# A start with x in order on one queue and TensorE filled, a reordered sixth pair, and scan results ahead of additions in the last part

## The chip, the cores and the metric

The kernel runs on one core of a Trainium2 chip. The metric is the device time of one execution in microseconds (us). Three runs of the kernel before gave 1817.42, 1815.12 and 1814.30 us; their median, 1815.12 us, is the time before.

## The reference

The input x has 4 images of 128 channels and 96 x 96 points. Each image is normalized in 32 groups of 4 channels (mean and variance over the group's channels and all points). The normalized image is read as four sequences of 9216 points: by rows, by rows backwards, by columns, by columns backwards. Each sequence goes through one block with the same weights:

```
t = grouped1x1(x, in_proj, 4 groups)            # 128 -> 512 channels
u, gate = t[:256], t[256:]
u = conv1d(silu(u), 5 taps, each channel by itself)
s = ssm_in u;  bb = tanh(B u);  cc = tanh(C u)  # 32 channels each
a = DMIN + (DMAX - DMIN) * sigmoid(delta u)
h[l] = a[l] * h[l-1] + bb[l] * s[l]             # a scan along the sequence
u = u + ssm_out (cc * h + d * s)
y = out_proj (grouped1x1(u * sigmoid(gate), mix))
```

The four results are put back into image order, joined to 512 channels, multiplied with fuse_w (128 x 512), and x is added.

## The kernel before, in words

**Tiling.** The work is cut into 384 units. Two units, s = 0 (forward) and s = 1 (backward), make a pair, and `pair(t)` is called for t = 0 to 191. A batch element has two phases of 24 pairs: V (by columns) and H (by rows). A phase has 6 steps (st) of 4 pairs (p, or k). A unit covers 384 points (every fourth point of 16 lines). In the first three steps of a phase (`fresh`) the input projection and the gates are computed; in the last three the forward and backward units change places and the stored results are read back from DRAM (`load_silu`, `load_kept`).

**One pair.** `pair(t)` (line 784 on) has a front part for units 2t and 2t+1 and a back part for the pair LAG = 6 earlier, so that pairs 0 to 5 have no back part and pair 6 is the first that has one. On TensorE the order is: `front` (the input projection `in_proj` of the step after, four products into four PSUM banks, followed by four Silu on ScalarE, line 470), `conv` and `conv_less` (the convolution of half of the channels as products with diagonal matrices), an `accumulate` of a finished unit (the product with w_fin, line 729 on), `gates_and_out` (gates line 491, scan result times ssm_out line 504), a second `accumulate`, and `proj` (the products with w_proj). The other half of the channels is convolved on VectorE: `taps`, tap 0 on ScalarE (line 635) and taps 1 to 4 on VectorE (line 637), all through one pair of PSUM banks. `recurrence` does the scan on VectorE (line 709, two halves per step) and `outputs` (lines 715 and 716, then a copy) multiplies it by cc and adds the d * s term on GpSimd; d * s is `scale_s` on ScalarE (line 692). `gating` (lines 583 and 584) multiplies with the gate on VectorE. `sigmoids` (line 521) evaluates the gates on ScalarE. `accumulate` ends in an addition into `acc` (line 761), which is the output image of the batch element, held in SBUF and preloaded with x: on GpSimd from a copy `ys`, or on VectorE straight from PSUM where `direct` is set.

**What sets the order.** The program runs under a manual schedule: each engine executes its instructions in the order in which the program text issues them. SyncE (SP) issues nearly all DMAs in that order on one queue.

**The opening**, `start()` (line 996) and the lines before it. `load_x` (line 294) asks for the first image in ten DMAs of 1, 1, 1, 2, 2, 3, 4, 4, 4 and 2 chunks of 384 points, with one `bn_stats` on VectorE per chunk (line 298). After these come the weights `fuse` (512 KB) and `main` (384 KB), two loads of `x_in` for step 0 (385 KB each) and eight for the gates, all on SP's queue; only `small` is asked for from ScalarE. `stats_finish(b0)` turns the statistics into the scaled weights `wn` and biases `bn` over four small products, with TensorE kept busy by `filler` products (line 1000) and by the products `outer` (line 1007) and `inner` (line 1015), from which w_fin is made. Then sixteen Silu, one per s, block j and g, in the order of j = 0 and then j = 1, with two buffers of `x_in` that serve step 0 and step 1 alike, so that the loads of step 1 (`load_rows`) follow the products of step 0. `proj(0)` issues the front of step 1 itself.

**Statistics of later images.** `chunks_of` (line 372) names the chunks of the next image that a V pair loads and gives to `bn_stats` (line 387): two in each pair with k of 2 or 3, in all six steps, with four buffers `xs`.

**The end**, `tail()` (line 905): for the last six pairs (first = 186) it issues gating, the last scan, four `outputs`, and an alternation of `product`, `add` and `ssm_out`.

Of the kernel before, what the change touches and what calls it, by code (L numbers as in the profile page):

```python
# [67 lines left out]
def conv_preact_kernel(  # L68
# [18 lines left out]
    accf = acc.rearrange("p h r m -> p (h r m)")  # L87
    x_in = [big.tile([P, R, N + 1], F32, name=f"x_in{s}") for s in range(2)]
# [65 lines left out]
    gmask = wp.tile([P, 4], F32, name="gmask")  # L154
    nc.gpsimd.memset(gmask, 1.0)
# [13 lines left out]
    stats, free = {}, [FRONT[1]]  # L169
# [10 lines left out]
    def stats_finish(b):  # L180
# [12 lines left out]
        nc.vector.tensor_copy(mean, pm[:, 0:1])  # L193
        dev = sp.tile([P, 1], F32, tag="dev", name=f"dev_{b}")
        nc.vector.tensor_sub(dev, mv[:, 0:1], mean)
        ex = sp.tile([P, 1], F32, tag="ex", name=f"ex_{b}")
        nc.vector.scalar_tensor_tensor(ex, dev, dev, mv[:, 1:2], ALU.mult, ALU.add)
        gm4 = sp.tile([P, 4], F32, tag="gm4", name=f"gm4_{b}")
        nc.vector.tensor_scalar_mul(gm4, gmask, mean)
# [9 lines left out]
        if b == b0:  # L209
# [4 lines left out]
            nc.vector.reciprocal(inv, std)  # L214
        else:
# [11 lines left out]
        yield  # L227
# [11 lines left out]
        product(pb[:, 0:4], wn, gm4)  # L239
        if b == b0:  # L240
            for g in range(4):
                for q in range(R):
                    mm(pb[:, 4 + g : 5 + g], q, wn[0:32, 32 * g : 32 * g + 32], mean[0:32, :], True, True)
            nc.vector.tensor_sub(bn, b_in, pb[:, 0:8])
        else:
# [10 lines left out]
        nc.vector.tensor_scalar_mul(bn[:, 2:4], bn[:, 2:4], 0.5)  # L256
# [8 lines left out]

    def load_front(step, s, r, q):
        if fresh(step):
            un = units[step * UB + s]
            nc.sync.dma_start(
                x_in[s][r, q, :], xs[un["b"], un["lay"], r, q, bass.ds(un["st"] * N, N + 1)]  # L270
            )
# [22 lines left out]
    def load_x(chunks):  # L294
        for c, n in chunks:
            nc.sync.dma_start(accf[:, bass.ds(c * SC, n * SC)], xr[b0, :, bass.ds(c * SC, n * SC)])
            for e in range(c, c + n):
                nc.vector.bn_stats(stats_of(b0)[:, e, :], accf[:, bass.ts(e, SC)])
# [6 lines left out]
    nc.scalar.activation(first_table, first_table, AF.Sqrt)  # L305
    w_small = load(small, "small", nc.scalar)
    load_x([(0, 1), (1, 1), (2, 1), (3, 2), (5, 2), (7, 3), (10, 4), (14, 4), (18, 4), (22, 2)])
    w_out_fuse = load(fuse, "fuse")
    w_main = load(main, "main")
    for s in range(2):  # L310
        load_front(0, s, half(s), slice(0, R))
    for i in range(UB):
        load_gate(i)
# [29 lines left out]
    for s in range(2):  # L343
# [14 lines left out]
    nc.gpsimd.tensor_scalar_mul(  # L358
        w_proj[:, :, 2 * MH : 3 * MH], w_proj[:, :, 2 * MH : 3 * MH], 0.5
    )  # L360
# [3 lines left out]
    gates = [wk.tile([P, 2, 2, N], F32, tag=f"gate{e}", bufs=1, name=f"gate{e}") for e in range(2)]  # L364
# [7 lines left out]
    def chunks_of(t):  # L372

        un = units[2 * t]
        b, k = un["b"] + 1, t % R
        if un["order"] == "V" and b < B and k > 1:
            return [(b, un["st"] * R + 2 * (k - 2) + e) for e in range(2)]
        return []

    def load_chunks(t):  # L380
        for b, c in chunks_of(t):
            chunks[b, c] = wk.tile([P, SC], F32, tag="xs", bufs=4, name=f"xs_{b}_{c}")
# [78 lines left out]
    def in_proj(step, g, s, j, bk):  # L461
        wn = stats[units[step * UB]["b"]][0]
        r = slice(64 * s + 32 * j, 64 * s + 32 * j + 32)
        for c in range(4):
            m, q = (c, g) if j else (g, R - 1 - c if s else c)
            mm(bank(bk), c, wn[r, s, 32 * m : 32 * m + 32], x_in[s][r, q, :], True, True)

    def silu(step, g, s, j, bk):
# [3 lines left out]
            bank(bk)[:, : N + 1],  # L472
            AF.Silu,
# [40 lines left out]
    def sigmoids(bi, to):  # L514
# [3 lines left out]
        for s in range(2):  # L518

            for j in (0, 1) if s == 0 or to[0] == GATE[True][0] else (1, 0):  # L520
# [30 lines left out]
    def gates_and_out(bi, with_front):  # L551

        to = GATE[with_front]
# [19 lines left out]
    def gating(bi, s):  # L573
# [8 lines left out]
        if bi not in seeded:  # L582
            nc.vector.tensor_add(pz, pz, v)
# [13 lines left out]
    def conv(i, banks):  # L597
# [3 lines left out]
        for s in range(2):  # L601
# [21 lines left out]
    def taps(i, ks, first=None):  # L623
# [4 lines left out]
        part = psum[:, TAPS : TAPS + 2, :N]  # L628
        for k in ks:
# [6 lines left out]
            else:  # L636
                nc.vector.scalar_tensor_tensor(  # L637
                    us[i][:, :, 1, :] if k == K - 1 else part,
# [9 lines left out]

    def proj(i, banks, apart=False):
# [8 lines left out]
        turns = [(e, j) for j in ((1, 0) if i else (0, 1)) for e in range(2)]  # L658
        apart = apart or not i
        for e, j in sorted(turns) if apart and i else turns:  # L660
            if i == 0 and (e, j) == (0, 0):
                first = front_parts(R, (5, 4, 2, 3), half=True)
                next(first)
                next(first)
                first_tap(2)
                for _ in first:
                    pass
            for c, cols in enumerate(((qb, qb, qa, qa), (qs, qs, qc, qc))[e]):
                first, end = (j == 0, j == 1) if apart else (j == 1, j == 0)
                mm(bank(banks[e]), c, w_proj[:, j, cols], us[i][:, c % 2, j, :], first, end)  # L670
# [19 lines left out]
    def scale_s(i):  # L690
        s = tbs[i][0:64, :]
        nc.scalar.activation(s, s, AF.Copy, scale=d_sb[0:64, 0:1])
# [91 lines left out]
    def pair(t):  # L784
# [13 lines left out]
        if back:  # L798
# [13 lines left out]
        if t:  # L812
            new_u(i)
            taps(i, range(1, K))
            conv(i, banks)
        if t and not ahead:
            conv_less(i, banks)
        if not back and t:
# [86 lines left out]
    def tail():  # L905
# [35 lines left out]
        ssm_out(first + 1)  # L941
        for held_add in adds:
# [3 lines left out]
        outputs(2 * first + 8, None)  # L946
# [4 lines left out]
        outputs(2 * first + 10, None)  # L951
# [44 lines left out]
    def start():  # L996
        w_of = wp.tile([P, 4, 2, P], F32, name="w_of")

        def filler(n):
            nc.tensor.matmul(  # L1000
                bank(7)[:, :n], accf[:, bass.ds(10 * SC, P)], accf[:, bass.ds(10 * SC, n)],
# [3 lines left out]
        def outer(d, i, copy):  # L1005
# [175 lines left out]
```

## Time and profile before

| what | us |
|---|---|
| median of three runs | 1815.12 |
| the profiled execution's own time | 1815.66 |
| its span, first to last instruction | 1813.9 |
| TensorE busy | 1788.7 |
| ScalarE busy | 1562.6 |
| VectorE busy | 1448.5 |
| GpSimd busy | 1431.1 |
| granted TensorE clock, mean | 0.999 |

The span is one profiled execution; 1.8 us of its own time lie outside it. A group of instructions has a line of the kernel, an engine, what it writes and reads, a shape, how often it ran, its busy time, and the idle time ahead of it with what ended that. PE is TensorE, PEld its weight loads, DVE VectorE, ACT ScalarE, POOL GpSimd, SP SyncE. TensorE is nearly always busy in this page, but the ends of matrix products are modelled, so idle time of TensorE is better read from the start times of successive products.

### The profile page before, as it was taken

How to read it: one execution, taken by the hardware profiler on the slowest of the kernel's cores; microseconds unless marked ns; L12 is line 12 of the kernel's file. 1: busy time of each engine (PE TensorE's matmuls, PEld its weight loads, DVE VectorE, ACT ScalarE, POOL GpSimd, SP SyncE). 2: the span in 40 equal slices, each digit the busy share in tenths (PEclk: the TensorE clock that was granted, in tenths of full speed). 3: DMA queues.
4: the chain of work that ended last, by engine and by line, in shares of the span. 5: the costliest groups of instructions: out<-in, count | busy, mean ns of one | idle time of the engine just before them, and what ended most of it. 6: DMA issues, size and time to landing. Idle time of an engine off the chain costs nothing.

```text
span 1813.9 us, 56969 instructions
## 1 busy us (share of the span) xinstructions
PE 1788.7 (99%) x24090; PEld 643.7 (35%) x24090; DVE 1448.5 (80%) x1462; ACT 1562.6 (86%) x2750; POOL 1431.1 (79%) x1477
## 2 busy tenths in 40 slices
PE   7999999999999999999999999999999999999998
PEld 3333333333333333333333333333333333333333
DVE  6888878787888887877778888787877788777886
ACT  4888888988888888898888888889888888888975
POOL 3587888788778888787877888878877788887786
PEclk9999999999999999999999999999999999999999
DMA  8555463444975466344696456443476634635434
GB/s 247 178 188 180 148 195 107 162 144 155 314 239 186 158 186 183 113 139 139 221 300 226 144 176 207 127 164 118 159 237 220 232 142 138 197 102 180 149 123 158
DMA packets 148047, 321.17 MB, mean 177 GB/s; under 512 B 14160, under 2 KB 115920, under 8 KB 147792
## 3 DMA queue, kind: packets, MB, share of 16 engines
q1 hardware_dynamic: 147648, 317.48, 54.1%
q8 instruction: 190, 3.11, 0.7%
q14 instruction: 65, 0.53, 0.1%
q10 hardware_dynamic: 144, 0.04, 0.0%
HBM read 185.21 MB, written 132.25 MB: 175 GB/s over the span
## 4 chain that ended last, share of the span: by engine, by line
PE 94%; DVE 2%; DMA 2%; ACT 1%; issue 0%; POOL 0%; SPq 0%; DVEq 0%; ACTq 0%; POOLq 0%
PE psum L134 81%; PE psum L504 8%; PE psum L491 5%; DVE psum L637 1%; DMA x_in<-in_xs 1%; DMA xs<-in_xr 1%; DVE u L584 0%; DMA acc<-in_xr 0%; DVE u L637 0%; ACT psum L635 0%; ACT psum L512 0%; ACT u L618 0%; ACT sil L470 0%; DVE t L715 0%; DVE t L709 0%
## 5 line engine op out<-in xcount | busy, mean ns | idle before, releaser
L637 DVE SCALAR_TENSOR_TENSOR psum<-sil,small,psum 128x768 f32<-128x768 f32 x576 | 589.0, 1022 | 28.3 <-ACT psum L635 3.4
L584 DVE SCALAR_TENSOR_TENSOR u<-gate,psum 128x768 f32<-128x768 f32 x376 | 349.6, 952 | 273.9 <-ACT u L616 122.4
L134 PE MATMUL psum<-u,w_fin 128*32 128x384 f32 (+1 forms) x6192 | 552.7, 486 | 3.5 <-DVE acc L761 2.1
L134 PE MATMUL psum<-u,main 128*32 128x384 f32 x6144 | 534.7, 489 | 1.2 <-DVE u L637 1.2
L761 POOL TENSOR_TENSOR acc<-ys,acc 128x384 f32<-128x384 f32 x375 | 411.7, 1119 | 27.9 <-ACT ys L744 8.4
L715 POOL TENSOR_TENSOR t<-t,t 64x384 f32<-64x384 f32 (+1 forms) x192 | 237.3, 1236 | 157.0 <-DVE t L709 73.3
L134 PEld LDWEIGHTS psum<-u,w_fin 128*32 128x32 f32 x6192 | 189.7, 110 | 322.6 <-issue 215.2
L134 PEld LDWEIGHTS psum<-u,main 128*32 128x32 f32 x6144 | 181.9, 109 | 324.5 <-issue 196.8
L512 ACT COPY psum<-u 128x768 f32<-128x768 f32 x352 | 276.8, 799 | 19.2 <-DVE u L637 11.3
L134 PE MATMUL psum<-sil,band 128*32 128x384 f32 x3072 | 285.1, 488 | 0.0
L682 POOL TENSOR_SCALAR t<-tm 64x384 f32<-64x384 f32 x191 | 177.0, 926 | 118.1 <-ACT tm L674 98.9
L716 POOL TENSOR_TENSOR t<-t,t 64x384 f32<-64x384 f32 (+1 forms) x192 | 248.8, 1296 | 15.1
L504 PE MATMUL psum<-t,main 32*128 32x384 f32 x1536 | 239.2, 513 | 1.3 <-ACT psum L512 0.6
L635 ACT ACTIVATE psum<-sil,small 128x768 f32<-128x768 f32 x191 | 173.2, 907 | 58.0 <-DVE u L584 49.7
L521 ACT ACTIVATE gate<-psum,bnorm 128x384 f32<-128x384 f32 x384 | 191.7, 581 | 27.0 <-PE psum L491 25.5
L683 POOL TENSOR_TENSOR t<-t,tm 64x384 f32<-64x384 f32 x192 | 195.1, 1016 | 15.3
L637 DVE SCALAR_TENSOR_TENSOR u<-sil,small,psum 128x768 f32<-128x768 f32 x192 | 194.9, 1015 | 7.8
L470 ACT ACTIVATE sil<-psum,bnorm 128x385 f32<-128x385 f32 x384 | 191.8, 584 | 3.9 <-PE psum L134 1.8
L134 PE MATMUL psum<-sil,less 64*32 64x384 f32 x3072 | 168.2, 495 | 0.0
L491 PE MATMUL psum<-x_in,wn 32*128 32x384 f32 x768 | 157.5, 527 | 0.4 <-ACT u L616 0.4
L134 PEld LDWEIGHTS psum<-sil,band 128*32 128x32 f32 x3072 | 90.6, 109 | 169.2 <-issue 95.0
L718 POOL COPY t<-t 64x384 f32<-64x384 f32 x187 | 136.5, 730 | 11.9
(102 smaller groups left out, 1477.2 us busy)
## 6 DMA issues: line engine op xcount, KB each, us to landing
sil<-sil SPq DMA_DIRECT2D x128, 770.0 KB, 6.9
kept<-gate SPq DMA_DIRECT2D x80, 768.0 KB, 3.7
gate<-kept SPq DMA_DIRECT2D x76, 768.0 KB, 4.8
x_in<-in_xs SPq DMA_DIRECT2D x192, 96.2 KB, 2.5
out<-acc SPq DMA_DIRECT2D x48, 384.0 KB, 8.5
acc<-in_xr SPq DMA_DIRECT2D x39, 384.0 KB, 6.4
xs<-in_xr SPq DMA_DIRECT2D x72, 192.0 KB, 5.8
x_in<-in_xs SPq DMA_DIRECT2D x46, 192.5 KB, 3.5
```

Source lines behind the costliest of these rows:

```text
L134: nc.tensor.matmul(o[r, : rhs.shape[-1]], lhsT, rhs, start=start, stop=stop, skip_group_check=True)
L470: nc.scalar.activation(sils[step][:, s, j, g, :], bank(bk)[:, : N + 1], AF.Silu, bias=bn[:, 1:2] if j else bn[:, 4 + g : 5 + g],)
L491: nc.tensor.matmul(bank(to)[:, :N], stats[un["b"]][0][r, s, :], x_in[s][r, q, off : off + N], start=True, stop=True)
L504: nc.tensor.matmul(bank(ssm(bi, s) + j)[:, :N], w_so[r, bass.ts(j, P)], z[r, :], start=bi not in seeded, stop=True, skip_group_check=True)
L512: nc.scalar.copy(psum[:, ssm(bi, s) : ssm(bi, s) + 2, :N], us[bi][:, s])
L521: nc.scalar.activation(gv[:, s, j, :], bank(to[2 * s + j])[:, :N], AF.Tanh, bias=bn[:, 2 + j : 3 + j], scale=0.5,)
L584: nc.vector.scalar_tensor_tensor(v, g, 1.0, pz, ALU.add, ALU.mult)
L637: nc.vector.scalar_tensor_tensor(us[i][:, :, 1, :] if k == K - 1 else part, src, w_tap[:, k : k + 1], part, ALU.mult, ALU.add,)
L683: nc.gpsimd.tensor_mul(ta[0:64, p, :], tb[0:64, :], tm[0:64, :])
L715: engine.tensor_mul(ta[0:64, p, r], tb[64:P, r], ta[64:P, p, r])
L716: engine.tensor_add(tb[0:64, r], ta[0:64, p, r], tb[0:64, r])
L761: adder.tensor_add(part, y, part)
```

## The change

The change has these parts.

**Loads.** A function `loads` asks for x in nine DMAs of 1, 2, 3, 4, 4, 4, 3, 2 and 1 chunks on SP, and for `fuse` on ScalarE's queue at once. Behind x come the first third of `main`, the step-0 loads into a tile of their own, `x_first`, the rest of `main`, the step-1 loads into `x_in`, and the gates. The second gate buffer shares the memory of `x_first`.

**Opening.** All `outer` products and one `inner` come ahead of the statistics' end; the fillers read late chunks of x, and the bias product `b_final` stands between them. In the statistics' chain of the first image the deviation is taken from PSUM, and the bias product uses the unscaled weights with a mean that is already scaled. A Silu covers both s (`both_silus`, 770 elements); the order of blocks is (1,0), (0,0) to (0,3), (1,1) to (1,3). Unit 0's taps go through SBUF, in the order 0, 4, 1, 2, 3; tap 0 of unit 2 is done on VectorE. `front(R)` ends the opening, and `proj(0)` has the order of all others.

**Pairs 1 to 5.** `scale_s` goes to GpSimd. No statistics chunks are loaded or read in steps 0 and 1 of any V phase; steps 2 to 5 take three chunks per pair with k of 2 or 3, with six buffers.

**Pair 6.** Half of the front's Silu go behind the convolution's copies, the four `out_of` products ahead of the four gates, the banks are others, and the two additions of `gating` ahead of its two multiplications.

**Tail.** `outputs(2 * first + 8)` goes ahead of the two held additions, and `outputs(2 * first + 10)` ahead of the products of the pair `first`.

```diff
-        nc.vector.tensor_copy(mean, pm[:, 0:1])
         dev = sp.tile([P, 1], F32, tag="dev", name=f"dev_{b}")
-        nc.vector.tensor_sub(dev, mv[:, 0:1], mean)
+        nc.vector.tensor_sub(dev, mv[:, 0:1], pm[:, 0:1])
...
+        nc.vector.tensor_copy(mean, pm[:, 0:1])
...
+            nc.vector.tensor_scalar(gm4, gmasks, mean, inv[:, 0:1], ALU.mult, ALU.mult)
...
-        product(pb[:, 0:4], wn, gm4)
+        product(pb[:, 0:4], w_in[:, 0, :] if b == b0 else wn, gm4[:, 0:4])
...
-    load_x([(0, 1), (1, 1), (2, 1), (3, 2), (5, 2), (7, 3), (10, 4), (14, 4), (18, 4), (22, 2)])
-    w_out_fuse = load(fuse, "fuse")
-    w_main = load(main, "main")
...
+    def loads():
+        nc.scalar.dma_start(w_out_fuse, fuse)
+        nc.scalar.activation(first_table, first_table, AF.Sqrt)
+        ask_x((0, 1), (1, 2), (3, 3), (6, 4), (10, 4), (14, 4), (18, 3), (21, 2), (23, 1))
+        nc.sync.dma_start(w_main[:, 0:HID], main[:, 0:HID])
+        for s in range(2):
+            load_front(0, s, half(s), slice(0, R))
+        nc.sync.dma_start(w_main[:, HID:], main[:, HID:])
+        for s in range(2):
+            load_front(1, s, half(s), slice(0, R))
+        for i in range(UB):
+            load_gate(i)
+        for c in range(NSC):
+            nc.vector.bn_stats(stats_of(b0)[:, c, :], accf[:, bass.ts(c, SC)])
...
-        if un["order"] == "V" and b < B and k > 1:
-            return [(b, un["st"] * R + 2 * (k - 2) + e) for e in range(2)]
+        if un["order"] == "V" and b < B and k > 1 and un["st"] > 1:
+            return [(b, 3 * (2 * un["st"] + k - 6) + e) for e in range(3)]
...
+    def both_silus(step, g, j, b0):
+        bn = stats[units[step * UB]["b"]][1]
+        nc.scalar.activation(
+            sils[step][:, :, j, g, :],
+            psum[:, b0 : b0 + 2, : N + 1],
+            AF.Silu,
+            bias=bn[:, 1:2] if j else bn[:, 4 + g : 5 + g],
+        )
...
-        to = GATE[with_front]
+        to = GATE[with_front] if bi else (4, 5, 7, 6)
+        if bi == 0:
+            for s in range(2):
+                for j in range(2):
+                    out_of(bi, s, j)
+            for s in range(2):
+                for j in range(2):
+                    gate(bi, s, j, to[2 * s + j])
+            sigmoids(bi, to)
+            return
...
-        if bi not in seeded:
+        if bi == 0 and s == 0:
+            for e in range(2):
+                pe = psum[:, SSM + 2 * e : SSM + 2 * e + 2, :N]
+                nc.vector.tensor_add(pe, pe, us[bi][:, e])
+        elif bi and bi not in seeded:
             nc.vector.tensor_add(pz, pz, v)
...
         s = tbs[i][0:64, :]
+        if i < 2 * LAG - 2:
+            nc.gpsimd.tensor_scalar_mul(s, s, d_sb[0:64, 0:1])
+            return
...
-        if back:
+        if bi == 0:
+            turned = front_parts(t + R, (2, 3, 7, 6), half=True)
+            next(turned)
+            next(turned)
+        elif back:
             front(t + R, FRONT)
...
+        if bi == 0:
+            for _ in turned:
+                pass
...
         ssm_out(first + 1)
+        outputs(2 * first + 8, None)
         for held_add in adds:
             held_add()
         gate_units(first + 1)
         outputs(2 * first + 6, None, nc.vector)
-        outputs(2 * first + 8, None)
+        outputs(2 * first + 10, None)
         product(first, 0, 4)
         product(first, 1, 5)
         z_copy(first + 2)
         product(first + 1, 0, 4)
-        outputs(2 * first + 10, None)
         add()
...
+        loads()
+        for d in range(4):
+            outer(d, (0, 1, 4, 5)[d])
...
         pieces = stats_finish(b0)
...
+        inner((2, 3), 2)
+        inner_copy(nc.scalar, (2, 3), 2)
+        for c in (14, 14, 18, 18):
+            filler(c)
+        b_final()
+        filler(22)
+        filler(22, 256)
         next(pieces)
-        for n in (512, 512):
-            filler(n)
         next(pieces)
-        outer(0, 0, nc.scalar.copy)
-        outer(1, 1, nc.scalar.copy)
+        filler(18, 256)
         next(pieces)
-        outer(2, 4, nc.scalar.copy)
+        filler(18)
         next(pieces)
...
+        order = [(1, 0)] + [(0, g) for g in range(R)] + [(1, g) for g in range(1, R)]
+        spots = (D, A, C, D, A, C, A, C)
...
+        for n in range(3):
+            burst(*order[n], spots[n])
+        silus(*order[0], D)
+        burst(*order[3], D)
+        taps(0, (0,), nc.vector, spare=True)
+        taps(0, (R,), last=3, spare=True)
...
+        front(R, (5, 4, 2, 3))
```

## The prediction

> **What bounds the kernel now.** I read the page first, then busy time by stretches, the chain that ended last, and the timelines of both ends.
>
> ```profile
> span 1813.9 us, 56969 instructions
> PE 1788.7 (99%) x24090; PEld 643.7 (35%) x24090; DVE 1448.5 (80%) x1462; ACT 1562.6 (86%) x2750; POOL 1431.1 (79%) x1477
> PE 94%; DVE 2%; DMA 2%; ACT 1%; issue 0%; POOL 0%; SPq 0%; DVEq 0%; ACTq 0%; POOLq 0%
> ```
>
> TensorE bounds it: 94% of the chain is TensorE, and none of its products in the 180 pairs between the ends is shortened here. So only the two ends can give something. The chain at the start and the first regular pairs:
>
> ```profile
> 3.17 6.94 DMA acc<-in_xr
> 10.13 13.85 DMA x_in<-in_xs
> 24.11 3.66 PE psum L134 x85
> ...
> 36.27 12.40 DMA xs<-in_xr
> ...
> 84.97 8.89 PE psum L134 x112
> ...
> 95.41 7.56 PE psum L134 x96
> ```
>
> The first 24 us are DMA, x and then the step-0 loads of x_in; a statistics chunk holds the chain from 36.27 to 48.67; from 78.92 on it is TensorE without a gap. All that the head can gain lies ahead of 79 us. Its timeline:
>
> ```profile
> 12.04 6.66 DVE L298 BATCH_NORM_STATS2 bn<-acc 128x6 f32<-128x384 f32 x14 [0.43 <-DMA acc<-in_xr]
> 24.11 3.66 PE L134 MATMUL psum<-x_in,wn 32*32 32x385 f32 x88 [0.32 <-DMA x_in<-in_xs]
> 25.02 5.30 ACT L470 ACTIVATE sil<-psum,bnorm 128x385 f32<-128x385 f32 x11 [0.59 <-PE psum L134]
> 48.70 1.06 DVE L387 BATCH_NORM_STATS2 bn<-xs 128x6 f32<-128x384 f32 x2 [2.03 <-DMA xs<-in_xr]
> 72.88 0.56 PEld L491 LDWEIGHTS psum<-x_in,wn 32*128 32x128 f32 x3 [1.02 <-ACT u L616]
> 78.92 0.88 PE L134 MATMUL psum<-x_in,wn 32*32 32x385 f32 x16 [0.57 <-DVE u L584]
> ```
>
> The last number in brackets is idle time and what ended it: statistics run to 18.70, the front waits for x_in to 23.98, pair 3's VectorE waits 2.03 for a chunk, pair 6 waits for a copy, pair 7 for gating. The end:
>
> ```profile
> 1787.54 2.81 DVE L715 TENSOR_TENSOR t<-t,t 64x384 f32<-64x384 f32 x1
> 1787.65 1.95 POOL L761 TENSOR_TENSOR acc<-ys,acc 128x384 f32<-128x384 f32 x2
> 1790.38 1.63 DVE L716 TENSOR_TENSOR t<-t,t 64x384 f32<-64x384 f32 x1
> 1791.94 0.54 DVE L761 TENSOR_TENSOR acc<-psum,acc 128x384 f32<-128x384 f32 x1
> 1792.53 4.33 PE L134 MATMUL psum<-u,w_fin 128*32 128x384 f32 x32 [2.14 <-DVE acc L761]
> ```
>
> TensorE waits 2.14 us for an addition that stands on VectorE behind two slow multiply-adds, and then needs 4.33 us where the same 32 records take 2.79 at 1797.65.
>
> [...] L715 (two SBUF inputs) ends at 1790.35, 0.75 after GpSimd's two additions end at 1789.60. [...] The trace shows both rates: fillers every 0.85 us until 17.35, then every 0.43; weight loads 0.64 apart after the 2.14 us wait, 0.32 otherwise. [...]
>
> **The change part by part.**
>
> *Loads.* Two rates of the DMA view price a piece (one partition's run): 417 GB/s at 12 to 16 us with 6144-byte pieces is 16 x 6144 / 417 = 236 ns on each of 16 engines, 228 GB/s at 20 to 24 us with 1540-byte pieces is 108. A straight line gives 1024 bytes 93, 1536 108, 3072 150, 4096 179, 4608 193. An engine moves 8 pieces of a 128-partition transfer. Before: x is 24 x 108 + 24 x 150 + 8 x 193 + 24 x 236 = 13.4 us; fuse 1.43; main 1.20; x_in 32 x 108 = 3.46; with 2.0 to the first byte, 0.5 for small and 1.5 to be seen (the lag behind the bytes in this view) 23.5, measured 23.98. After: x is 16 x 108 + 16 x 150 + 16 x 193 + 24 x 236 = 12.9, but fuse now shares its time, so x ends near 2.0 + 0.5 + 1.43 + 12.9 + 1.5 = 18.3 and the last bn_stats (0.54) near 18.9, against 18.70: no gain. The front needs only a third of main, 8 x 93 = 0.74, so it lands 0.5 + 0.46 = 1.0 earlier, at 23.0. Bounds: 22.0, if fuse fills the gaps of the first 5 us; 24.2, if nothing comes of it.
>
> *Statistics' chain.* bn_aggr to wn took 18.74 to 22.44. One copy (0.19) leaves the chain, and the biases no longer wait for wn. With the last bn_stats at 18.9, aggregation ends near 19.75; the bias is ready some 3.3 later, 23.1. Fillers: 5.5 x 0.85 = 4.7 us if warm. They need x chunks from 14 on and so start near 13.5, end near 19.7 and cost nothing if the outer products have warmed TensorE; cold they cost twice that (rival 2). So the front starts at 23.1; by the 0.91 us from the first full burst (24.11) to its Silu (25.02), the first Silu starts at 24.0.
>
> *Silu.* Sixteen cost 0.48 each. One over 770 elements is estimated from copies of 384 and 768 (0.47 and 0.80): 0.58 + 0.33 = 0.91, at a pitch of 0.81. Eight take 6.5 us, plus 0.4 for TensorE's bursts (8 x 0.66 and two inner pieces, nearly as long). The last ends at T = 30.9; before, 32.60. The inner products leave the path (1.98 at 27.77), the early taps are covered by Silu, and only tap 3 (1.02) follows T.
>
> *Pairs 0 to 6.* I compare starts of proj, read from the timeline. After T come tap 3 and the front of step 1 together: start at T + 1.35 = 32.25, against 35.34. TensorE's own cycle, where least is waited for, is 5.76 (pairs 4 to 5); I use 5.75, and 6.05 for the first. The scale on GpSimd (about 0.93 there, by L682) takes 0.62 from ScalarE, busy 9.64 of 10 us at 60 to 70; GpSimd is busy 4.54 there, so it costs nothing; nor does it gain, since TensorE's cycle remains. Scans in pairs 4 and 5 (1.8 each) bring VectorE to 6.05, which its lead covers.
>
> Starts of proj, before against after: pair 1 41.59, 38.3; pair 2 47.44, 44.05; pair 3 54.00, 49.8; pair 4 59.84, 55.6; pair 5 65.60, 61.35. The chunks that are gone are the 0.8 us of pair 3. Pair 6: before it took 9.15; its products need 8.5, and the wait of 0.7 goes, since copies now precede half of the Silu and the scan products need no copied bank. 74.75 becomes 69.85, 4.9 us. Both additions of gating can start about 1.3 us earlier, so pair 7's wait (78.92, where 78.07 would follow) goes: 0.85. **Head: 5.75 us**; bounds 2.5 and 8.
>
> *Chunks elsewhere.* A third bn_stats (0.51) in 24 pairs. VectorE works 6.07 us in the pair at 114 to 123, of about 9.11, and idles 2.06 before gating: nothing. If it were the bound, rival 3. The SP queue issues one more load in such pairs; chunks came in 3.2 to 7.0 us and have two pairs' time.
>
> *Tail.* GpSimd ends outputs of pair 188 at 1787.68. L715 has shown a gap of 0.07 to 0.09 ahead of it each time (1789.60 to 1789.67), in which a waiting VectorE came in. With outputs(2 first + 8) next, VectorE's L715 runs to 1788.43, GpSimd's to 1789.6, VectorE's L716 to 1790.2, the addition to 1790.75. TensorE, done at 1790.40, goes on at 1790.85 instead of 1792.53 and stays warm: 1.68 + 1.54 = **3.2 us**. Moved behind: the held additions (2 x 0.98), for which only `ys` buffers wait, and these are next asked for near 1794. Moved earlier: outputs of pair 191, not waited for. Bounds: a loss of 1.5, if VectorE's addition has to wait for the held ones; a gain of 3.6.
>
> **Sum.** 5.75 + 3.2 = 8.95. The profiled execution's 1815.66 becomes 1806.7; it lies 0.54 above the median, so 1815.12 becomes **1806.2**.
>
> **Rivals.** 0.2%, 3.6 us, is about what can be told from no change.
> 1. *The tail gives nothing*: [...] the addition waits for the held ones. For it: at 1787.65 GpSimd did win. Against: the gaps above. 1809.4 to 1811; 1809.9.
> 2. *Fillers overrun*: TensorE is cold and four of 5.5 fillers take 1.7 us, so the first statistics product starts 3.4 us late, and the front with it. For it: before, it was cold until 17.35. Against: outer products start some 6 us earlier. 1806.2 + 3.3 = 1809.5.
> 3. *Slower*: VectorE becomes the bound of the V pairs with three chunks. 24 x 0.51 = 12.2 us; from 1806.2 it gives 1818.4. It decides if fewer than 0.5 us per pair are idle; 2.06 speaks against it.
> 4. *The opening does not do what it says*: x and x_in land no earlier, the Silu are bound by TensorE, and only pairs 3, 6 and 7 gain (0.8 + 0.65 + 0.85), with no tail: 1812.8.
>
> **Numbers.** Forecast 0.58 (its own range 1803.5 to 1808.5), rival 1 0.18, rival 2 0.14, rival 3 0.05, rival 4 0.05. Of rival 1 some 0.03 lies within 0.2% of before (above 1811.5), so faster is 0.58 + 0.15 + 0.14 = 0.87, same 0.08, slower 0.05. Range 1803.0 to 1811.5: it leaves out rivals 3 and 4, 0.03 of rival 1 and about 0.05 below.
>
> **What would show it.** x_in seen near 23.0 and the first Silu near 24.0; proj of pair 0 near 32.25, of pair 6 near 69.85; no wait of TensorE in pair 7; regular pairs of 9.11 us unchanged; GpSimd and VectorE taking turns near 1788 and weight loads 0.32 apart after 1790. It is wrong if fillers still run after bn_aggr ends, if VectorE enters the chain in pairs with chunks, or if TensorE still waits 2 us for the addition.

## The result and the profile after

The changed kernel took 1813.3 us (median of 22 runs) against 1815.7 us for the kernel before beside it (22 runs): a ratio of 0.9982, 95% interval 0.9975 to 0.9988. It is faster, by about 2.4 us, where 8.9 us were predicted, and it lies above the range. Its executions lie in groups, 15 from 1812.5 to 1815.0 and six from 1809.4 to 1811.2; one more, of 2252 us at a granted clock of 0.76, stands outside both and outside the ratio. The profiled one took 1813.0 us of its own time, 2.7 below the profiled one of before.

The first lines of the page and its sum of the chain:

```profile
span 1811.1 us, 57008 instructions
PE 1793.5 (99%) x24112; PEld 645.5 (36%) x24112; DVE 1443.2 (80%) x1453; ACT 1563.6 (86%) x2738; POOL 1441.5 (80%) x1491
PE 96%; DVE 2%; ACT 1%; DMA 1%; issue 0%; SPq 0%; DVEq 0%
```

TensorE's share of the chain grew from 94 to 96% and DMA's fell: `x_in` is off the path at the start. But busy TensorE grew too, by 4.8 us, though it has only 22 products more. Part of them ran slower. The chain at the start:

```profile
3.21 10.20 DMA acc<-in_xr
...
37.40 11.55 PE psum L135 x192
49.00 23.82 PE psum L135 x379
```

The statistics chunk (`xs`) and `x_in` are gone from it; from 37.40 on it is TensorE. Yet 37.40, the proj of pair 0, is 2.06 us later than before. Lines of the timeline of the opening show why (start, busy time, and in brackets idle time and what ended it):

```profile
18.17 0.80 DVE L190 BATCH_NORM_AGGREGATE mv<-bn 128x2 f32<-128x144 f32 x1
19.12 0.24 PE L135 MATMUL psum<-mv,gmean 128*32 128x1 f32 x8
21.85 0.48 PE L135 MATMUL psum<-x_first,wn 32*32 32x385 f32 x1
22.95 4.08 ACT L500 ACTIVATE sil<-psum,bnorm 128x770 f32<-128x770 f32 x5 [0.62 <-PE psum L135]
26.15 0.85 PE L135 MATMUL psum<-x_first,wn 32*32 32x385 f32 x9
28.11 0.85 PE L135 MATMUL psum<-x_first,wn 32*32 32x385 f32 x7 [1.11 <-issue]
29.02 0.91 ACT L500 ACTIVATE sil<-psum,bnorm 128x770 f32<-128x770 f32 x1 [1.99 <-PE psum L135]
30.04 2.82 PE L135 MATMUL psum<-x_first,wn 32*32 32x385 f32 x32
31.68 0.91 ACT L500 ACTIVATE sil<-psum,bnorm 128x770 f32<-128x770 f32 x1 [1.76 <-PE psum L135]
32.96 0.91 ACT L500 ACTIVATE sil<-psum,bnorm 128x770 f32<-128x770 f32 x1 [0.38 <-PE psum L135]
```

Down to 22.95 all is earlier than predicted. Then a burst of 16 products is cut in two, 9 and 7, with 1.11 us of idle time ended by "issue", which means by nothing that the profile shows. After it 32 products take 2.82 us, where 1.67 were enough at 23.90. ScalarE waits 1.99, 1.76 and 0.38. Stretches of 10 us (length, then busy time and instructions of PE, PEld, DVE, ACT and POOL, then granted clock, DMA share, GB/s):

```profile
20.00:30.00 10.00, 8.63 (x162) 3.92 (x162) 3.29 (x10) 6.68 (x9) 1.35 (x10) 0.94 1.00 245
30.00:40.00 10.00, 9.96 (x129) 2.85 (x132) 8.43 (x10) 4.86 (x8) 0.00 (x0) 0.72 0.91 229
40.00:50.00 10.00, 9.96 (x178) 3.23 (x173) 4.25 (x6) 8.22 (x16) 5.16 (x5) 1.00 0.17 38
```

The clock is 0.72 on the mean from 30 to 40. In the clock record it is half from 28.84 to 35.67, 6.83 us, twice 3.413. The end of the kernel, by contrast:

```profile
1788.35 0.88 DVE L756 TENSOR_TENSOR t<-t,t 64x384 f32<-64x384 f32 x1
1788.57 1.74 POOL L756 TENSOR_TENSOR t<-t,t 64x384 f32<-64x384 f32 x1
1789.26 1.69 DVE L757 TENSOR_TENSOR t<-t,t 64x384 f32<-64x384 f32 x1
1790.39 1.56 POOL L757 TENSOR_TENSOR t<-t,t 64x384 f32<-64x384 f32 x1
1790.87 0.54 DVE L802 TENSOR_TENSOR acc<-psum,acc 128x384 f32<-128x384 f32 x1
1791.47 2.79 PE L135 MATMUL psum<-u,w_fin 128*32 128x384 f32 x32 [0.26 <-DVE acc L802]
```

VectorE's multiply takes 0.88 us instead of 2.81, TensorE's wait falls from 2.14 to 0.26, and its 32 products take 2.79 instead of 4.33.

Set side by side, starts of proj before and after: pair 0 35.34, 37.40; pair 3 54.00, 54.76; pair 4 59.84, 60.92; pair 6 74.75, 75.61; pair 7 86.28, 85.83. So the head gave 0.45. From there to the last proj (1775.85, 1776.67) 1.27 were lost, of which 0.67 in pair 76 and 0.35 in pair 104. In pair 76 TensorE again stops in the middle of a burst with "issue" (its weight loads for 0.54 us, up to 718.67). From the last proj to the end 3.6 were gained, and the two gains at the lines above, 1.88 and 1.54, are 3.4 of them. 0.45 - 1.27 + 3.6 = 2.8, as the spans of 1813.9 and 1811.1 have it.

### The profile page after: what moved, and what is told of

It is laid out like the page before. It is cut to its first block, busy times and chain, and to the rows that moved or that the text cites. A ratio compares the mean times of both kernels' runs of the same rounds, so it can differ in the third digit from the quotient of the medians.

```text
span 1811.1 us, 57008 instructions
## 1 busy us (share of the span) xinstructions
PE 1793.5 (99%) x24112; PEld 645.5 (36%) x24112; DVE 1443.2 (80%) x1453; ACT 1563.6 (86%) x2738; POOL 1441.5 (80%) x1491
## 3 DMA queue, kind: packets, MB, share of 16 engines
q8 instruction: 190, 3.11, 0.7%
## 4 chain that ended last, share of the span: by engine, by line
PE 96%; DVE 2%; ACT 1%; DMA 1%; issue 0%; SPq 0%; DVEq 0%
PE psum L135 83%; PE psum L534 8%; PE psum L521 5%; DVE psum L680 1%; DMA acc<-in_xr 1%; DVE u L627 0%; PE psum L1053 0%; DVE u L680 0%; ACT psum L542 0%; ACT u L661 0%; SPq L307 0%; PE psum L1068 0%; ACT ys L785 0%; ACT t L715 0%; ACT psum L678 0%
## 5 line engine op out<-in xcount | busy, mean ns | idle before, releaser
L756 POOL TENSOR_TENSOR t<-t,t 64x384 f32<-64x384 f32 (+1 forms) x192 | 237.8, 1238 | 156.0 <-DVE t L750 72.2
L627 DVE SCALAR_TENSOR_TENSOR u<-x_first,psum 128x768 f32<-128x768 f32 x188 | 175.0, 953 | 140.7 <-ACT x_first L551 65.9
L627 DVE SCALAR_TENSOR_TENSOR u<-gate,psum 128x768 f32<-128x768 f32 x188 | 175.0, 953 | 127.7 <-ACT u L659 67.0
L757 POOL TENSOR_TENSOR t<-t,t 64x384 f32<-64x384 f32 (+1 forms) x192 | 249.2, 1298 | 15.1
L491 ACT ACTIVATE sil<-psum,bnorm 128x385 f32<-128x385 f32 x368 | 184.5, 585 | 2.2
```

Of the source, the lines that this page charges most:

```text
L491: nc.scalar.activation(sils[step][:, s, j, g, :], bank(bk)[:, : N + 1], AF.Silu, bias=bn[:, 1:2] if j else bn[:, 4 + g : 5 + g],)
L627: nc.vector.scalar_tensor_tensor(v, g, 1.0, pz, ALU.add, ALU.mult)
L756: engine.tensor_mul(ta[0:64, p, r], tb[64:P, r], ta[64:P, p, r])
L757: engine.tensor_add(tb[0:64, r], ta[0:64, p, r], tb[0:64, r])
```

## The suspect

My theory for the stop: TensorE had run out of instructions. The DMA record has, beside the data, 190 packets of 16 KB on a queue of their own (the page names it "instruction"), 3.11 MB in all; the trace has 48,761 TensorE records, nearly all a weight load or a product each, and 3.11 MB / 48,761 is 64 bytes, so that by my estimate a packet is 256 records. No record shows when a packet is asked for; I take the 256th record as a mark near it, since in the kernel before the first packet starts 0.31 us behind that record, beside DMA engines that are 0.07 busy. The rows below are worked out from the records of all the runs told of here, in us on the same zero as the lines of the profile; in the expectations quoted further down, times of packets, records and clock stand 0.3 us later. Busy is the mean share of the DMA engines between the 256th record and the packet's start (overlapping packets make it exceed 1). The next column counts the records issued when the packet had landed. The last two give how long after that landing the 450th record started, and how long after the 449th.

```
kernel        256th rec.  first packet    busy  records  450th: after landing, after 449th
before        24.82       25.13 to 26.24  0.07  333      3.83  0.00
after         21.86       25.53 to 26.76  1.08  449      1.35  1.59
opening_only  23.60       26.70 to 27.91  1.08  442      1.48  1.15
warm          21.91       25.41 to 26.67  1.08  435      1.42  0.30
fewer_pe      23.23       26.95 to 28.20  1.07  428      1.32  0.42
early_gates   22.17       23.92 to 25.28  1.07  394      2.44  0.00
queued_block  23.74       25.63 to 26.73  1.07  383      2.25  0.00
tail_only     24.50       24.86 to 26.46  0.13  367      3.28  0.01
gates_late    23.36       23.74 to 25.06  0.79  358      2.61  0.00
extra_load    25.16       25.48 to 26.82  0.07  357      3.59  0.00
short_fill    23.53       24.40 to 25.74  0.00  341      3.63  0.01
early_fill    21.63       22.10 to 23.08  0.00  330      4.10  0.00
late_fewer    25.06       25.49 to 26.88  0.00  324      3.73  0.00
late_loads    24.92       24.22 to 25.39  -     314      3.85  0.00
```

There is a stop wherever 428 records or more were out before the packet landed, and none up to 394. And the stop has one place: in all four kernels that have it TensorE issues 449 records, and the 450th follows 1.3 to 1.5 us after the packet has landed, although the 450th record is another product of the work in fewer_pe and in warm than in the other two. Where the 450th came 2.25 us or more after the landing, nothing stops, and in none of these 14 profiles does a record 450 + k x 256 start sooner than 1.3 us after its packet has landed. The stop of pair 76 fits as well: it stands after record 19,393, which is 449 + 74 x 256, and ends 1.55 us after a packet has landed. (Why the place is 449 was not shown. Nor is the 256th record more than a mark: in late_loads the packet started 0.7 us before it.) In the four with a stop the packet came 3.1 to 3.7 us late, while the DMA engines were full (1.07 or 1.08); where they were nearly empty (0.13 or less) it came within 0.9. The rivals: the stop is an effect of half clock, or of too many products.

## The experiments

Each run stood beside runs of the kernel before; ratios are to these. Of the variants of the changed kernel only early_gates has an interval that lies clear below the changed kernel's own (0.9975 to 0.9988), so it is the profiles, more than the times, that separate the others from it. "Held" loads are asked for after the second wide Silu.

**One half each.** *tail_only*: before, with the tail's order. *opening_only*: after, with the tail of before.

```diff
+        outputs(2 * first + 8, None)
         for held_add in adds:
             held_add()
...
-        outputs(2 * first + 8, None)
+        outputs(2 * first + 10, None)
```

> The kernel before with the order of the tail alone changed. The prediction's mechanism (VectorE's two multiply-adds come in between GpSimd's, so that TensorE's wait of 2.14 us shrinks and the clock stays full) gives 3.4 us by the two profiles: 1812.3. If the tail's gain came from the state in which the opening leaves the pairs, less than 1 us.

> The changed kernel with the tail's order of before. If the tail is worth the 3.4 us of the profiles and the rest of the change nothing, 1813.3 + 3.4 = 1816.7, that is 1 us slower than before; the prediction's sum would have it near 1809.5.

tail_only 1813.39, ratio 0.999 (0.9981 to 0.9999); opening_only 1815.56, 0.9993 (0.9983 to 1.0003). In medians -2.1 and -0.4, together about the 2.4 of the whole; why the median of tail_only shows less than the 3.4 expected was not found. The tail of tail_only:

```profile
1790.61 0.54 DVE L761 TENSOR_TENSOR acc<-psum,acc 128x384 f32<-128x384 f32 x1
1791.21 2.79 PE L134 MATMUL psum<-u,w_fin 128*32 128x384 f32 x32 [0.26 <-DVE acc L761]
```

The same durations as in the changed kernel, and a span of 1811.0. So the tail does what was forecast in the profile; the opening as a whole is worth nothing that can be told from zero.

**late_loads**: after, with step-1 and gate loads held (a small memset in `x_in` makes them wait).

```diff
-        for s in range(2):
-            load_front(1, s, half(s), slice(0, R))
-        for i in range(UB):
-            load_gate(i)
...
         silus(*order[1], A)
+        for s in range(2):
+            nc.gpsimd.memset(x_in[s][64 * s : 64 * s + 32, :, 0:1], 0.0)
+        for s in range(2):
+            load_front(1, s, half(s), slice(0, R))
+        for i in range(UB):
+            load_gate(i)
         burst(*order[4], A)
```

> The changed kernel with one difference: the step-1 loads of x_in and the gate loads are issued only after the second wide Silu of the opening, not behind x. Theory F (instruction load): TensorE's next block of instructions, asked for when record 256 is executed (22.2 us), waits behind these loads until 25.8 us, TensorE runs dry from 27.0 to 28.1, and the idle stretch makes the clock halve for 6.8 us. Then here the block's load starts within 0.5 us of record 256, the 1.1 us gap is gone, the clock stays full and the last wide Silu ends near 30 us instead of 33.9; time near 1813.3 - 1.1 - 3.0 = 1809. Rival H (the stretch is bound by Silu, and TensorE is too idle there whatever its instructions do): the gap goes, but the clock still halves for two windows; time near 1812.

1809.45, ratio 0.9962 (0.9949 to 0.9975). The packet comes at 24.22, and the stop is gone:

```profile
13.54 6.69 PE L1049 MATMUL psum<-acc 128*128 128x512 f32 x8 [2.48 <-DMA acc<-in_xr]
25.99 5.09 ACT L496 ACTIVATE sil<-psum,bnorm 128x770 f32<-128x770 f32 x6 [0.60 <-PE psum L135]
31.62 1.70 ACT L496 ACTIVATE sil<-psum,bnorm 128x770 f32<-128x770 f32 x2 [0.54 <-PE psum L135]
```

Eight Silu take 7.33 us instead of 10.92. But in this execution the first is 3 us late: the fillers waited 2.48 us for chunk 14, the clock was half from 12.76 to 19.58, and the first statistics product started at 22.19. That is the prediction's second rival, seen in one execution of a kernel other than the one it was written for.

**fewer_pe**: after, with `b_final` in 3 products of 128 columns instead of 12 of 32. **warm**: after, with short fillers of 128 or 256 columns in the Silu stretch.

```diff
+            full = slice(0, P)
...
-            for c in range(4):
-                for n, (lhsT, rhs) in enumerate(terms):
-                    mm(pf, c, lhsT[:, 32 * c : 32 * c + 32], rhs, n == 0, n == 2)
+            for n, (lhsT, rhs) in enumerate(terms):
+                nc.tensor.matmul(pf, lhsT[:, full], rhs, start=n == 0, stop=n == 2)
```

```diff
+        warm(0, 256)
         silus(*order[0], D)
         burst(*order[3], D)
+        warm(0, 128)
...
```

> The changed kernel with b_final made of 3 products over 128 columns instead of 12 over 32, which takes 36 records from TensorE ahead of the opening's Silu; loads as in the change. Theory F: record 256 comes later in the work, and the gap moves some 36 records (about 0.9 us of work) later and shrinks to 0.3 us or less; half clock in fewer executions; 1810 to 1812. Rival H: the gap shrinks and the time stays near 1813.

> The changed kernel with seven short filler products (128 to 256 columns on the full array) between the bursts of the opening's Silu stretch; loads as in the change. Theory F: the gap of about 1.1 us stays, as the load is late all the same, and comes up to 28 records earlier in the work; the clock may halve once instead of twice; 1811 to 1813.5. Rival H: the clock stays full and the time is near 1810.

fewer_pe 1809.35, 0.9965 (0.9954 to 0.9977); warm 1811.42, 0.9975 (0.9962 to 0.9987). In warm the clock is full from 11.35 on, and still (the 12 weight loads behind the stop, and the Silu that waits):

```profile
28.10 0.17 PEld L135 LDWEIGHTS psum<-x_first,wn 32*32 32x32 f32 x12 [0.52 <-issue]
29.05 0.90 ACT L500 ACTIVATE sil<-psum,bnorm 128x770 f32<-128x770 f32 x1 [1.60 <-PE psum L135]
```

A stop at full clock refutes the first rival: half clock is not its cause. It may be the other way: with the long stops of the changed kernel and opening_only (1.59 and 1.15 us in the table) the clock falls, with filler work around the stop it doesn't. But the stop of warm is also shorter, 0.30, so warm alone does not tell the work from the length. In fewer_pe, which came out below its 1810 to 1812, the packet is as late as ever (3.7 us), but fewer records lie ahead of it: TensorE stops for 0.42, and ScalarE waits 1.26 for it.

**late_fewer** and **short_fill**: late_loads and fewer_pe in one; and that with 2.5 fillers instead of 5.5.

```diff
-        for c in (14, 14, 18, 18):
+        for c in (14, 18):
             filler(c)
         b_final()
-        filler(22)
         filler(22, 256)
```

> Both edits on the changed kernel: step-1 and gate loads after the second wide Silu, and b_final from 3 products of 128 columns. Theory F: with the late loads no instruction load waits any more, so taking 36 records out adds little: 1808.5 to 1809.5, like each edit alone. Rival (each edit removes a cost of its own): near 1805.5.

> As late_fewer, with 2.5 fillers instead of 5.5 ahead of the first statistics product (chunks 14 and 18 with 512 columns, 22 with 256). The two profiles with a halved clock at 13 us show that product at 20.26 and 22.19, with bn_aggr done at 18.8 and 19.1; if fillers that run on at half clock are what still costs, the product follows bn_aggr by 0.2 us whatever the clock does, the executions lie closer together, and the time is 1806 to 1808. If the fillers' clock is needed for the Silu stretch, the clock halves there and it is 1809 or more.

late_fewer 1810.37, 0.9974 (0.9963 to 0.9984): no better than either, and above what was expected; its profiled execution has the clock at half from 12.86 to 19.69, as late_loads has. short_fill 1809.25, 0.9978 (0.9968 to 0.9987), but its executions range from 1808.5 to 1816.0, in two groups with 5.4 us between them. The granted clock is 0.997 or 0.998 in the lower group and 0.992 to 0.994 in the upper, so the upper has more of half clock; the profile is of the lower (half from 12.63 to 22.87), and where the upper has it was not seen. Leaving fillers out is no cure.

**extra_load** and **queued_block**: the kernel before with four more loads of 385 KB, behind the gate loads and ahead of them (from DRAM into a tile in SBUF that nothing reads, not to DRAM, as one expectation says).

```diff
+    extra = [dp.tile([P, R, N + 1], F32, tag=f"extra{e}", name=f"extra{e}") for e in range(2)]
+    for e in range(2):
+        for s in range(2):
+            r = slice(64 * s, 64 * s + 64)
+            nc.sync.dma_start(extra[e][r], xs[1, e, r, :, 0 : N + 1])
```

> The kernel before with four extra DMAs of 385 KB from DRAM to DRAM behind the gate loads (they compute nothing that is used), so that the DMA queue is still full when TensorE's next block of instructions is asked for. Theory F: that block's load, which starts 0.3 us after record 256 in before (25.44), starts 2 us or more late, and TensorE shows a gap without a releaser of up to 1 us [...], besides a later landing of the step-1 rows; 1816 to 1821. If instruction loads don't wait for data loads, the block starts near 25.5 as before and only a wait for step-1 rows appears.

> The kernel before with the same four 385 KB loads as in extra_load, but ahead of the gate loads instead of behind them, so that their bytes stand in the DMA queue when TensorE reaches its 256th record (25.1 us). Theory (the block of instructions waits behind queued loads): the first block starts at 28.5 to 32 instead of 25.4, TensorE runs dry after about 430 records, near 29.5 to 30, and stops for 1 to 3 us inside the Silu stretch with nothing in the profile that ends the wait; with one or two half-clock windows the median is 1821 to 1827. Rival (the block comes when it is asked for, and the stop in the changed kernel had another cause): block at 25.4 to 26, no stop in the Silu stretch, and the time of extra_load, 1819 to 1821.5.

extra_load 1820.5, 1.0028 (1.0017 to 1.0039), but it missed its aim: the gate loads held SP until 24.8, so that the DMA engines were empty when the packet came, at 25.48. Its cost is a wait for step-1 loads behind the extra bytes:

```profile
37.02 2.47 PE L134 MATMUL psum<-x_in,wn 32*32 32x385 f32 x32 [2.48 <-DMA x_in<-in_xs]
```

queued_block 1816.15, 1.0003 (0.9994 to 1.0012), is half a hit. With the engines full (1.07) the packet came 1.9 us late instead of 0.3: the lateness is made by other bytes. But it did not wait until all loads were through: it landed at 26.73, and the DMA engines were still 0.8 busy at 28. (SP issued gate loads until 28.44; which of them were asked for ahead of the packet was not shown.) And as only 383 records were out, no stop came. What sets 1.9 here and 3.7 there stays open.

**gates_late**: after, with the gate loads alone held.

```diff
-        for i in range(UB):
-            load_gate(i)
...
         silus(*order[1], A)
+        for s in range(2):
+            nc.gpsimd.memset(x_in[s][64 * (1 - s) : 64 * (1 - s) + 32, :, 0:1], 0.0)
+        for i in range(UB):
+            load_gate(i)
         burst(*order[4], A)
```

> The changed kernel with only the gate loads held until the second wide Silu; the step-1 loads stay where the change put them. By the queue theory the block of instructions starts when the queue is empty, so some 1.7 us (385 KB at 228 GB/s) before the 25.84 of the changed kernel, at 23.5 to 24.5, lands by 25.7, ahead of the record near 430 at which TensorE ran dry (26 to 27), and the stop is gone: Silu stretch of 7.3 to 8 us, median 1808.5 to 1810.5, about as with both held. If the step-1 loads alone are enough to delay it, the block stays at 25 to 26, the stop remains, and the median is 1812 to 1814.

1808.88, ratio 0.9972 (0.996 to 0.9983), on the first theory's numbers throughout: packet at 23.74, Silu from 24.43 to 31.76, 7.33 us. The DMA view from 22 to 26 us (40 slices; the 16 KB packet is the queue named instruction), first of the changed kernel, then of gates_late:

```profile
DMA  9799999999899999899998999979999998999999
q8 instruction: 1, 0.02, 1.9%
```

```profile
DMA  9999999999997998593000000000000000000000
q8 instruction: 1, 0.02, 2.1%
```

In the first the engines are full to the end; in the second they run empty by 23.9, and the packet starts at 23.74. All the products of the changed kernel are still in it, so the second rival fails too. Its proj of pair 0 starts at 33.79, 3.6 us ahead of the changed kernel, although its first Silu is 1.5 us later.

**early_fill**: late_fewer and two fillers on earlier chunks, in the pause that late_loads showed.

```diff
+        filler(6)
+        filler(10, 256)
         for c in (14, 14, 18, 18):
```

> The changed kernel with the step-1 and gate loads held until the second wide Silu, b_final in three products, and two more fillers, on chunk 6 (512 columns) and chunk 10 (256), ahead of those on chunk 14. They fill the pause of TensorE of 2.5 us that ended at 13.54 in late_loads, after which its clock stood at half from 13.07 to 19.89 and the fillers ran 3.1 us past bn_aggr. If that pause is what cools TensorE, the clock is full from 13 to 17 on in most executions, the first statistics product starts near 19.5 instead of 22.1, the first Silu near 23.5, and the median is 1807 to 1808.5 (late_loads 1809.45). If the phase of the clock's windows decides whatever TensorE does, it stays at 1809 to 1811; if the two fillers are only more work in a cold stretch, they end 2.5 us later and it is 1811 to 1813.

1808.83, 0.9967 (0.9954 to 0.9979), five runs within 1 us of each other. The clock is full from 11.72 on, and the first Silu starts at 22.51. The narrow spread speaks for the pause of 2.48 us as what the half clock of late_loads goes with. That is argued, not shown, and it is not the whole of it: in the profiled execution of the changed kernel, where TensorE paused for 1.49 us ahead of 13.46, the clock was full from 11.78 to 28.84 without these fillers. What part the phase of the clock's steps has was not shown. The median is just above the first theory's 1807 to 1808.5, and the wait that the next kernel shows is in it too.

**early_gates**: the edits of gates_late and fewer_pe, and the two fillers of early_fill, in one.

> The changed kernel with only the gate loads held, b_final in three products, and the two early fillers (gates_late and early_fill in one). The opening should lose nothing: no stop, clock full from about 13 to 17 on, first Silu near 22.5 to 23.5, proj of pair 0 at 31.5 to 32.7 and of pair 3 at 48.9 to 50.1, that is where the prediction had them. Theory (pair 4's front waits for loads of x_in that the earlier opening does not bring forward): proj of pair 4 starts at 57.2 to 58.0 all the same, as in gates_late (57.58), early_fill (57.65) and short_fill (57.69), TensorE waits 1.2 to 2.5 us there, and the median stays at 1808 to 1809.2. Rival (pair 4's wait is an effect of step-1 or gate loads that were held, or moves with the opening): proj of pair 4 at 54.7 to 56.5, median 1806 to 1807.5.

1807.54, ratio 0.9951 (0.9937 to 0.9964): ahead of both kernels. TensorE's timeline:

```profile
32.42 2.79 PE L135 MATMUL psum<-u,main 128*32 128x384 f32 x32
38.17 2.79 PE L135 MATMUL psum<-u,main 128*32 128x384 f32 x32
44.02 2.79 PE L135 MATMUL psum<-u,main 128*32 128x384 f32 x32
49.77 2.79 PE L135 MATMUL psum<-u,main 128*32 128x384 f32 x32
55.47 1.61 PE L135 MATMUL psum<-x_in,wn 32*32 32x385 f32 x32 [0.82 <-DMA x_in<-in_xs]
57.01 2.79 PE L135 MATMUL psum<-u,main 128*32 128x384 f32 x32
```

These are the prediction's 32.25, 38.3, 44.05 and 49.8 to within 0.2, but for pair 0 that is in part luck: the first Silu starts at 23.05 instead of 24.0, the stretch takes 7.34 instead of 6.9, and proj follows its end (30.39) by 2.03 instead of 1.35. With the packet in time and the clock full, the opening gives what was forecast as a sum. Then pair 4 starts at 57.01, not 55.6: its front waits for `x_in`. In gates_late it starts at 57.58. Against it pair 0 is 1.37 earlier, pair 4 only 0.57. So neither expectation holds whole: pair 4's start moves, but by less than half of what the opening gains, TensorE waits 0.82, and the median is 0.5 below the theory's range and at the edge of the rival's. The loads it waits for are issued by SP from 49.83 to 53.36, after pair 3's front has read the buffers, and the last two, of 192.5 KB, need 3.4 us to land.

## Why the prediction was wrong in size

**The tail: right.** Forecast 3.2; 3.4 in the profile (1.88 of wait and 1.54 of products), and 2.1 in medians (tail_only). The order that was forecast came: GpSimd's L757 ends at 1788.49, its next operation starts at 1788.57, and VectorE's L756 (1788.35 to 1789.23) takes 0.88 us, where in the kernel before the same operation took 2.81 beside GpSimd's two additions (1787.65 to 1789.60). GpSimd's L756 at 1788.57, beside VectorE's two, takes 1.74; the one at 1793.97, with VectorE idle, takes 1.19. So the multiply of GpSimd's did not hold VectorE's up. The addition ended at 1791.41; forecast was 1790.75 for an execution level with before, and this one was 0.8 behind it there (GpSimd's L757 ends at 1788.49, against 1787.68).

**Loads and statistics: right, on the safe side.** Both `x_first` seen by 21.85 (23.0 forecast, 22.0 its bound), aggregation from 18.17, first Silu at 22.95 (24.0). Rival 2 is not in this execution: the first statistics product started at 19.12, 0.15 after the aggregation.

**The step that failed: "The last ends at T = 30.9".** It was worked as "8 x 0.81 plus 0.4 for TensorE's bursts", 6.9 us. With nothing in the way it is 7.33 (gates_late, early_fill, late_loads): 0.4 mis-sized, as is the 1.35 from there to proj, which is 2.03 in gates_late and early_gates. In the changed kernel the stretch is 10.92, and the half clock goes on to 35.67, past it: 37.40 for the proj of pair 0 against 32.25, that is -1.05 for the first Silu, +4.02 for the stretch and +2.18 for what follows it. The sum priced the loads that were moved up by when their own readers would get them. Who else uses the DMA engines, TensorE's instructions, was priced at nothing. Between 21.9 and 25.5 the engines carry the step-1 loads, which before were asked for only at 26.4, and behind them the gate loads, which before had landed by then; the packet waits; the stop of 1.1 us follows, and with it 6.83 us of half clock, by my estimate worth up to half of that, 3.4. gates_late, which moves one group of loads alone, gives 3.6 at pair 0. That the gate loads behind step 1's delay the packet, and that the stop goes with the delay, is shown. That the half clock follows from the stop is argued: it comes behind the two long stops (the changed kernel, opening_only), and neither behind the two short ones (warm, fewer_pe) nor where there is none (gates_late, early_gates).

**A second step that failed: the 5.75 us cycle in pair 4.** "TensorE's own cycle, where least is waited for" was carried over to all early pairs. Pair 3 to 4 takes 7.24 in early_gates, where the front waits for `x_in`. That is most of the 1.4 missing from the 5.75 us forecast for the head: 86.28 - 81.89 = 4.39 were had at pair 7. In the changed kernel it costs little (6.16), because the opening is late anyway.

**Pairs 3, 6 and 7, regular pairs: right in the sum.** From pair 2 to 3 the chunks' 0.8 is gone (6.56 to 5.76). From pair 5 to 7 it takes 19.15 against 20.68, 1.5 less, the 0.65 + 0.85 of the forecast, but the parts are not: pair 6 gives 0.22 (8.93 us against the 8.5 forecast) and pair 7 gives 1.31. That the two come out as forecast together is luck; why pair 6 takes 8.93 was not pursued. From pair 8 on only pairs 76 and 104 differ from before by more than 0.03 us, and VectorE's third statistics chunk costs nothing there, so rival 3 did not happen. Rival 4's number, 1812.8, is near the result, but not its reason: x and `x_in` did land earlier.

**Numbers.** 1806.7 was forecast for the profiled time, 1813.0 came: head 5.3 worse, 1.27 lost between, the end 0.4 better. Pair 76's 0.67 goes with its own stop and is not found in gates_late, early_gates or early_fill; pair 104's 0.35 is found in all three, and its cause was not pursued.

## What to carry to other kernels

Loads that are moved up have more neighbours than their readers: here the instructions of the busiest engine came in 190 packets of 16 KB beside the data, and the first came 0.3 us behind the 256th record beside nearly empty DMA engines (before) and 3.7 us behind it beside full ones (after). So find where that engine's packets come, and leave the DMA queue a gap there. Idle time that ends in "issue" in the middle of a burst (1.11 us here) is the mark to look for. And a chain that gets shorter at its start must be followed to the next load whose buffer is freed by it, before its gain is carried through.

## What the hardware showed that I had not expected

- A packet of TensorE's instructions, 16 KB, took 1.0 to 1.6 us (the first of each kernel) and came up to 3.7 us after the 256th record beside full DMA engines. Where it was that late, the engine stopped after exactly 449 records, whatever product came next, and went on 1.3 to 1.5 us after the packet had landed.
- A stop among light products (32 rows, 32 columns), 1.1 us of idle time, was followed by 6.83 us of half clock, and in the kernel before a wait of 2.14 us in the tail went with 3.41 us of it (1792.29 to 1795.71). In these two executions the stretches of the clock record, but for the one that the end cuts off, are multiples of 3.413 us (3.413, 6.827, 17.067 and 1774.931), and the first at full clock starts at 17.36 before and at 11.78 after. By my estimate two such steps of half clock more or less are worth up to 3.4 us, more than the whole measured gain.
